# Loads of a second graph layer issued by the sync engine instead of the scalar engine, with a longer rest behind them

## The chip, the cores and the metric

The kernel runs on one core of a Trainium2 chip. A core has a tensor engine (PE, with its weight loads shown apart as PEld), a vector engine (DVE), a scalar engine (ACT), GpSimd (POOL) and a sync engine (SP). Each engine works through its own list of instructions in order; semaphores tie the lists together. DMA transfers are issued by an instruction on ACT, SP or POOL. The metric is the device time of one execution in microseconds (us): 2264.95 us before the change, the median of three runs (2263.04 to 2268.02).

## The reference, cut to what matters

A graph of 6250 nodes with 256 features and 106250 edges, sorted by their target node; 6250 of the edges are the nodes' own loops. Two layers follow one another. The first, a message network with gates, is not touched by the change. The second is an attention layer with four heads (H = 4, F = 64), called with the first one's rows:

```python
h = (x @ W).reshape(n, H, F)
a_src = jnp.sum(h * att_src[None], axis=-1)
a_dst = jnp.sum(h * att_dst[None], axis=-1)
e = jax.nn.leaky_relu(a_src[src] + a_dst[dst], 0.2)
m = jax.ops.segment_max(e, dst, num_segments=n)
ex = jnp.exp(e - m[dst])
denom = jax.ops.segment_sum(ex, dst, num_segments=n)
alpha = ex / (denom[dst] + 1e-16)
out = jax.ops.segment_sum(h[src] * alpha[..., None], dst, num_segments=n)
y = out.reshape(n, H * F) + bias + x
# layer norm with gamma and beta, relu; then x = layernorm(x + that)
```

## The kernel before, in words

**Tiles.** The edges lie in tiles of 128, one edge a partition. The loops are taken out and treated with the node itself; 782 tiles are left (`TC`). Seven tiles make a window (`WT`), 112 windows in all (`NW`), each with at most 64 target nodes (`SLOTS`). Two windows make a group, 56 groups (`NG`). For the scores, groups are taken in pairs, except the last four, 52 to 55, which stand alone (`pairs`).

**The second layer** is the block of `fast` from line 1734 on. Its main loop (line 1995) goes over steps t. At step t it emits, in this order:

- one gather on POOL (line 2002, the helper's line 1327): 128 rows of 260 numbers of the first layer's result, for the edges of tile t, into the ring `G` of ten windows;
- for tile k = t - 4, at certain places of a window, copies of the gathered logits on ACT: seven tiles of a window at its end (line 2024), the first tile of the next group for the group before (line 2016). The 112 copies of line 2024 stand in the order of the windows, so the copy of window w needs gathers 7w to 7w + 6 and all before;
- at the end of a pair, a start of `weights` (line 1807): turns the scores (line 1822), runs four scans over them for the maximum of each target's segment (lines 1829, 1830, 1839, 1840; they read `cut`), takes exponents (line 1853), and puts windows on the list `late`;
- one or two calls of `sum1` (line 1955): it takes a window of the list, weighs its rows (`weighted`: small DVE product line 1868, small ACT copy line 1873, large DVE product line 1874, which reads what line 1873 wrote), and emits one matmul that adds a tile into its group's sum (line 1983). With a group's first tile it loads that group's kept rows (line 1973, tile `k3`, ring of three). With the last it starts `finish`;
- `finish` (line 1881) works out a group's result over about a dozen steps: DVE and ACT in turn, `k3` read from line 1906 on, two layer norms (`normed`: ACT lines 1923, 1924 and 1929), then two stores by SP (line 1940), one for each window. Windows overlap, so each store waits for the one before it to land, and the first of a group waits for ACT's last line 1929 of that group.

**`Steps`** (line 1334) holds these chains. A `yield n` puts a chain to rest for n steps, in which other chains and the main loop emit their instructions. Nothing is measured in this: it is an order written down once, and each engine then follows its part of it.

**`ahead`** (line 1755) is what the change touches. For each pair it loads, for each of its groups, the slot of every edge, repeated over partitions (`dB`, two loads of 128 KB, line 1764, ring of three), and the segment marks (`cut`, line 1771, ring of three). It rests, then for each group compares `dB` with the slot numbers on DVE (line 1778), multiplies the result by the nodes' logits on PE (line 1782) and sums on DVE (line 1799). `aheads` starts it once a pair, every 28 steps (14 for the single groups). Its result is used by `weights` of the same pair, which starts 32 steps after `ahead` for a pair.

Of the kernel before, what the change touches and what calls it, by code (L numbers as in the profile page):

```python
# [1257 lines left out]
def fast(  # L1258
# [37 lines left out]
    nc = tc.nc  # L1296

    def at(ap, offset, dims):
        return bass.AP(tensor=ap.tensor, offset=ap.offset + offset, ap=dims)
# [9 lines left out]
    def windows_of(g):  # L1309
        return range(2 * g, 2 * g + 2)  # L1310
# [23 lines left out]
    class Steps:  # L1334
# [18 lines left out]
        def finish(self):  # L1353
            while self.chains:
                self.step()

    def half_of(w):
        return slice(SLOTS * (w % 2), SLOTS * (w % 2 + 1))
# [40 lines left out]
    def ring(pool, shape, dtype, name, n):  # L1399

        of = rings.setdefault((name, id(pool)), [[], 0])
        if len(of[0]) < n:
            of[0].append(pool.tile(shape, dtype, name=f"{name}_{len(of[0])}"))
        of[1] += 1
        return of[0][(of[1] - 1) % n]
# [17 lines left out]
    with (  # L1423
# [276 lines left out]
        for n in range(TC + LAG):  # L1700
            if n < TC:
                g, t = order[n]
# [19 lines left out]
            if n >= LAG:  # L1722
                g, t = order[n - LAG]
# [10 lines left out]
    with (  # L1734
# [15 lines left out]
        def tiles_in(g):  # L1750

            t0 = 2 * WT * g
            return range(t0, min(t0 + 2 * WT, TC)), range(t0, min(t0 + GS, TC))

        def ahead(pair, box):

            cut = ring(ep, [P, P + 1], F32, "cut", 3)
            of = ring(ep, [P, 2 * GS, 2 * H], F32, "of", 3)
            box.update(cut=cut, of=of)
            dBs = []  # L1760
            for g in pair:
                dB = ring(ep, [P, W8, P], BF16, "dB", 3)
                for w in windows_of(g):
                    nc.scalar.dma_start(
                        dB[half_of(w), :, :].rearrange("p j e -> p (j e)"),
                        at(slots, w * W8 * P, [[0, SLOTS], [1, W8 * P]]),
                    )
                dBs.append(dB)
            for i, g in enumerate(pair):
                n = len(tiles_in(g)[1])  # L1770
                nc.scalar.dma_start(
                    cut[i * GS * H : (i * GS + n) * H, :],
                    at(cuts, tiles_in(g)[0][0] * P, [[P, n], [0, H], [1, P + 1]]),
                )
            yield 5
            for i, (g, dB) in enumerate(zip(pair, dBs)):
                ohT = ring(ep, [P, W8, P], BF16, "ohT", 2)
                nc.vector.tensor_scalar(ohT, dB, slot_p, None, op0=OP.is_equal)
                yield 2
                pn = ring(ops, [P, 2, W8, 3, 2 * H], F32, "pn", 2)  # L1780
                for j in range(W8):
                    nc.tensor.matmul(
                        pn[:, :, j, :, :].rearrange("p s c a -> p s (c a)"),
                        ohT[:, j, :],
                        node3[:, g, :, :, :].rearrange("p s c a -> p s (c a)"),
                        start=True,
                        stop=True,
                    )
                yield 2
                o = i * GS  # L1790

                mid = pn.rearrange("p s j c a -> p (s j c) a")[:, WT * 3 : (WT + 2) * 3, :]
                n = len(tiles_in(g)[1]) - WT
                for o, parts in (
                    (o, pn[:, 0, :WT, :, :]),
                    (o + W8, pn[:, 1, 1:n, :, :]),
                    (o + WT, mid[:, None, :, :]),
                ):
                    nc.vector.tensor_reduce(
                        of[:, o : o + parts.shape[1], :],  # L1800
                        parts.rearrange("p j c a -> p j a c"),
                        axis=AX.X,
                        op=OP.add,
                    )
                yield 1
# [56 lines left out]
        def weighted(g, w, o, n, of, ex, top):  # L1862

            if g not in ohs:
                ohs[g] = ring(ep, [P, 2 * W8, SLOTS], F32, "oh1", 2)
                one_hot(ohs[g], 2 * g, 2 * W8)
            gw = ring(ep, [P, WT if n > 1 else 1, D + 2 * H], F32, f"gw{min(n, 2)}", 4)[:, :n, :]
            nc.vector.tensor_mul(  # L1868
                gw[:, :, HA:],
                top[:, o : o + n, :],  # L1870
                first[:, WT * w : WT * w + n, None].to_broadcast([P, n, H]),
            )
            nc.scalar.copy(gw[:, :, D:HA], ex[:, o : o + n, :])  # L1873
            nc.vector.tensor_mul(  # L1874
                gw[:, :, :D].rearrange("p j (h f) -> p j h f", h=H),
                of[:, :n, :D].rearrange("p j (h f) -> p j h f", h=H),
                ex[:, o : o + n, :, None].to_broadcast([P, n, H, F]),
            )
            return gw
# [73 lines left out]
        sums, queue, read, ohs, k3s, left, written = {}, [], set(), {}, {}, {}, []  # L1953

        def sum1():

            while late and len(queue) < 8:
                piece = late.pop(0)
                g, w, o, n = piece[:4]
                gw = weighted(*piece)  # L1960
                queue.extend((g, WT * w + j, gw[:, j, :]) for j in range(n))
            if not queue:
                return
            g, t, gw = queue[0]
            if g not in sums and g >= 2 and g - 2 not in read:
                return
            queue.pop(0)
            if g not in sums:
                sums[g] = ring(eps, [P, D + 2 * H], F32, "fps1", 2)
                left[g] = len(tiles_in(g)[1])  # L1970
                u = everyone
                k3s[g] = ring(fp, [P, 3, D], F32, "k3", 3)
                nc.scalar.dma_start(k3s[g][u, :, :].rearrange("p c f -> p (c f)"), kept[g, u, :])
            begins = left[g] == len(tiles_in(g)[1])
            left[g] -= 1
            j = t - 2 * WT * g
            if j == WT:
                to, ohj = everyone, ohs[g][:, WT : WT + 2, :].rearrange("p j s -> p (j s)")
            else:
                to, ohj = (slice(0, SLOTS), j) if j < WT else (slice(SLOTS, P), j + 1)  # L1980
                ohj = ohs[g][:, ohj, :]
            ends = left[g] == 0 or j in (WT - 1, TC - 1 - 2 * WT * g)
            nc.tensor.matmul(sums[g][to, :], ohj, gw, start=begins, stop=ends)  # L1983
            if left[g] == 0:
                run.start(finish(g, sums[g]), 1)

        def aheads():
            for pair in pairs:
                while run.now < 2 * WT * (pair[0] - (len(pair) == 1)):
                    yield 1  # L1990
                yield from ahead(pair, boxes[pair[0]])
# [3 lines left out]
        while t < TC + LAG or late or queue or run.chains:  # L1995
# [8 lines left out]
            if 0 <= k < TC:  # L2004
                w = k // WT
                g = w // 2
# [14 lines left out]
                if k == tiles_of(w)[0][-1]:  # L2021
# [3 lines left out]
                    if w == NW - 1:  # L2025
                        run.start(weights(pair, box))
            sum1()
            if len(queue) + W8 * len(late) > 3 * W8 or t % 7 == 0 or t >= TC - 4 * WT:
                sum1()
# [64 lines left out]
```

## Time and profile before

| | us |
|---|---|
| three runs | 2268.02, 2264.95, 2263.04 |
| the profiled execution, its own time | 2266.64 |
| its span, first to last instruction | 2264.7 |
| first gather of the second layer starts | 1213.78 |
| last gather of the second layer starts | 2198.24 |
| last instruction on POOL starts (the last store) | 2252.49 |

Busy shares of the whole span are PE 69%, DVE 55%, ACT 22% and POOL 67%. They average over two layers with different limits: in the second layer PE is busy for about half the time and DVE for three quarters. Instructions that only issue a DMA are not counted as busy[...]; the profile writes such a row with a q behind the engine's name (ACTq, SPq). A wait is written in brackets behind the instruction it held up, with the instruction that ended it.

### The profile page before, as it was taken

Reading aid. Unit: us, or ns where it says so; the run is one execution under the profiler, and the core shown is the slowest. Engines: PE = TensorE matmul, PEld = TensorE weight load, DVE = VectorE, ACT = ScalarE, POOL = GpSimd, SP = SyncE. Lnnn points to the kernel's source line nnn. Section 1 sums busy time; section 2 is a strip of 40 time slices with the busy share of each in tenths; the row PEclk is TensorE's granted clock in tenths of the full one; section 3 lists DMA queues with packets and bytes.
Section 4 is the critical chain, followed back from the end, with each engine's and each line's share of the span. In section 5 each row is a group of like instructions: output and inputs, shape, how many; then the busy total and the mean of one; then the engine's idle time right before and its main releaser. Section 6 shows DMA issues by size and latency. Waiting matters only on the chain. (4 is left out here: it accounts for less than half of the span.)

```text
span 2264.7 us, 22022 instructions
## 1 busy us (share of the span) xinstructions
PE 1556.6 (69%) x5722; PEld 776.5 (34%) x5722; DVE 1237.3 (55%) x3333; ACT 508.5 (22%) x1526; POOL 1525.5 (67%) x1603
## 2 busy tenths in 40 slices
PE   8996788888888888988992355554545545454563
PEld 5663233333333333333551222222323223232331
DVE  7552133333343333433541667777776877777785
ACT  3331012222122221222342112111111111211211
POOL 1304777777777777777764777777777777777760
PEclk9998788989999989898996676766767677676776
DMA  5335445554555554555553555555555555555540
GB/s 163 131 99 157 128 128 156 168 165 143 151 155 170 165 151 143 155 170 165 176 155 91 138 161 145 154 147 155 152 149 161 144 156 151 148 156 150 156 137 27
DMA packets 163409, 332.53 MB, mean 147 GB/s; under 512 B 42467, under 2 KB 74306, under 8 KB 163273
## 3 DMA queue, kind: packets, MB, share of 16 engines
q0 software_dynamic: 75968, 208.00, 33.9%
q1 hardware_dynamic: 64736, 82.92, 11.4%
q10 hardware_dynamic: 22569, 40.12, 5.9%
q8 instruction: 47, 0.77, 0.2%
q14 instruction: 89, 0.73, 0.1%
HBM read 278.79 MB, written 52.12 MB: 146 GB/s over the span
## 5 line engine op out<-in xcount | busy, mean ns | idle before, releaser
L1327 POOL DMA_INDIRECT G<-parts,fidx x782 | 747.1, 955 | 327.5 <-issue 219.0
L1327 POOL DMA_INDIRECT G<-rows,fidx x782 | 747.5, 956 | 240.5 <-issue 222.9
L1689 PE MATMUL fps<-G,oh 128*64 128x257 f32 (+1 forms) x1674 | 533.1, 433 | 137.1 <-DMA G<-parts,fidx 120.6
L1983 PE MATMUL fps<-gw,oh 128*64 128x264 f32 (+1 forms) x1674 | 433.0, 469 | 238.3 <-DVE gw L1874 238.3
L1983 PEld LDWEIGHTS fps<-gw,oh 128*64 128x64 f32 (+1 forms) x1674 | 229.1, 168 | 412.8 <-DVE gw L1874 254.8
L1689 PEld LDWEIGHTS fps<-G,oh 128*64 128x64 f32 (+1 forms) x1674 | 196.6, 151 | 445.5 <-DMA G<-parts,fidx 226.7
L1874 DVE TENSOR_TENSOR gw<-G,bank 128x1792 f32<-128x1792 f32 (+1 forms) x167 | 249.0, 1491 | 175.0 <-ACT gw L1873 173.5
L1495 DVE TENSOR_SCALAR kind<-fps 128x1 f32<-128x1 f32 x112 | 12.5, 153 | 311.1 <-PE fps L1689 311.1
L1542 PE MATMUL fpg<-faT,fWihT 128*128 128x512 f32 (+2 forms) x432 | 171.6, 521 | 0.2 <-DVE faT L1513 0.2
L1822 PE MATMUL turn<-fident,e 128*120 128x128 f32 (+2 forms) x30 | 13.5, 449 | 219.4 <-ACT e L2016 219.4
L1410 DVE TENSOR_TENSOR oh<-bank,fslot 128x1024 f32<-128x1024 f32 x112 | 136.0, 1214 | 2.2 <-ACT bank L1853 2.2
L1923 ACT ACTIVATE frs<-fmv,eps_c 128x1 f32<-128x1 f32 x112 | 33.0, 294 | 306.0 <-DVE fmv L1922 152.0
L1650 DVE COPY nd<-hr 128x4 f32<-128x4 f32 x56 | 10.8, 193 | 160.1 <-ACT hr L1629 160.1
L1205 PE MATMUL fpm<-fWrT,fhT 128*128 128x256 f32 x392 | 91.7, 388 | 5.1 <-DVE fms L1213 5.1
L1542 PEld LDWEIGHTS fpg<-faT,fWihT 128*128 128x128 f32 x432 | 71.2, 191 | 68.9 <-issue 59.3
L1191 PE MATMUL fph<-fxc,fWrT 128*128 128x512 f32 (+1 forms) x208 | 88.9, 580 | 4.7 <-DMA fWrT<-in_WrT_dram 4.7
L1929 ACT ACTIVATE fy<-fy,frs 128x256 f32<-128x256 f32 x112 | 67.2, 600 | 98.4 <-DVE gw L1868 52.9
L1822 PEld LDWEIGHTS turn<-fident,e 128*120 128x120 f32 (+2 forms) x30 | 5.0, 166 | 233.2 <-ACT e L2016 231.6
L1205 PEld LDWEIGHTS fpm<-fWrT,fhT 128*128 128x128 f32 x392 | 74.9, 194 | 23.8 <-DVE fms L1213 8.8
L1873 ACT COPY gw<-bank 128x28 f32<-128x28 f32 (+1 forms) x167 | 28.5, 171 | 227.6 <-DMA dB<-slots 103.6
L1625 PE MATMUL fpg<-Wx,fyT 128*128 128x264 f32 x224 | 77.0, 474 | 3.0 <-ACT fyT L1616 3.0
L937 POOL DMA_INDIRECT packed<-frame,place x21 | 20.9, 995 | 77.6 <-DVE frame L902 71.5
(237 smaller groups left out, 1791.3 us busy)
## 6 DMA issues: line engine op xcount, KB each, us to landing
kept<-keep SPq DMA_DIRECT2D x56, 384.0 KB
k<-kept ACTq DMA_DIRECT2D x56, 384.0 KB
dB<-slots ACTq DMA_DIRECT2D x112, 128.0 KB
loop<-parts SPq DMA_DIRECT2D x110, 128.0 KB
parts<-fms SPq DMA_DIRECT2D x49, 256.0 KB
G<-parts,fidx POOLq DMA_INDIRECT x782
G<-rows,fidx POOLq DMA_INDIRECT x782
rows<-hr SPq DMA_DIRECT2D x110, 65.0 KB
```

The lines of the kernel that those rows point to most:

```text
L1191: nc.tensor.matmul(ph[:, :cols], WrT_s[:, r, k, m * P : (m + 1) * P], xc[:, k, :cols], start=(k == 0), stop=(k == 1),)
L1205: made = nc.tensor.matmul(pm[:, r, :], hT[:, r, k, j * P : (j + 1) * P], WrT_s[:, r, k, :], start=(k == 0), stop=(k == 1),)
L1327: nc.gpsimd.indirect_dma_start(out=to_tile, out_offset=None, in_=table, in_offset=bass.IndirectOffsetOnAxis(ap=idx, axis=0),)
L1410: nc.vector.tensor_tensor(to[:, :nj, :], iota_s[:, None, :].to_broadcast([P, nj, SLOTS]), of[:, :, None].to_broadcast([P, nj, SLOTS]), op= ...
L1542: nc.tensor.matmul(pg[:, :cols], WihT_s[:, k, c * P : (c + 1) * P], aT[:, k, :cols], start=(k == 0), stop=(k == 1),)
L1625: nc.tensor.matmul(ph[u, :], hs[i][:, k, u], Wx[:, k, :], start=(k == 0), stop=(k == 1))
L1689: nc.tensor.matmul(sums[g][to, :], ohj, got[t], start=begins, stop=ends)
L1873: nc.scalar.copy(gw[:, :, D:HA], ex[:, o : o + n, :])
L1874: nc.vector.tensor_mul(gw[:, :, :D].rearrange("p j (h f) -> p j h f", h=H), of[:, :n, :D].rearrange("p j (h f) -> p j h f", h=H), ex[:, o ...
L1923: nc.scalar.activation(r, mv[u, k, 1:2], AF.Ln, bias=eps_c[u])
L1929: nc.scalar.activation(y, y, AF.Identity, bias=m, scale=r)
L1983: nc.tensor.matmul(sums[g][to, :], ohj, gw, start=begins, stop=ends)
```

## The change

Three load instructions move from the scalar engine's list to the sync engine's: the slots (line 1764, 112 loads), the segment marks (line 1771, 56 loads) and the kept rows (line 1973, 56 loads). The rest behind the loads in `ahead` grows from 5 steps to 8. No line is added, so the line numbers stay.

```diff
@@ ahead @@
                 for w in windows_of(g):
-                    nc.scalar.dma_start(
+                    nc.sync.dma_start(
                         dB[half_of(w), :, :].rearrange("p j e -> p (j e)"),
                         at(slots, w * W8 * P, [[0, SLOTS], [1, W8 * P]]),
                     )
...
                 n = len(tiles_in(g)[1])
-                nc.scalar.dma_start(
+                nc.sync.dma_start(
                     cut[i * GS * H : (i * GS + n) * H, :],
                     at(cuts, tiles_in(g)[0][0] * P, [[P, n], [0, H], [1, P + 1]]),
                 )
-            yield 5
+            yield 8
@@ sum1 @@
                 k3s[g] = ring(fp, [P, 3, D], F32, "k3", 3)
-                nc.scalar.dma_start(k3s[g][u, :, :].rearrange("p c f -> p (c f)"), kept[g, u, :])
+                nc.sync.dma_start(k3s[g][u, :, :].rearrange("p c f -> p (c f)"), kept[g, u, :])
```

## The prediction

> **What bounds the kernel now.** The chain of waits came first; it stops at the last store and tells nothing. Then came busy time by stretch (columns: length, PE, PEld, DVE, ACT, POOL, each with its count, granted clock, DMA share, GB/s) and who waited for whom from 1250 us on (us in total, times, longest).
>
> ```profile
> by line: POOL out_dram L1942 0.0%; issue 0.0%; POOLq L1244 0.0%
> ...
> 1400.00:1600.00 200.00, 100.90 (x458) 56.78 (x459) 151.83 (x381) 38.22 (x157) 151.56 (x160) 0.68 0.55 150
> 1800.00:2000.00 200.00, 103.01 (x464) 57.84 (x464) 150.53 (x375) 38.16 (x156) 151.69 (x159) 0.70 0.56 152
> ...
> DVE gw L1874 <- ACT gw L1873: 173.5, 152, 5.2
> ACT gw L1873 <- DMA dB<-slots: 103.6, 25, 4.5
> POOL G L1327 <- issue: 213.3, 700, 0.3
> ```
>
> POOL makes 160 gathers in each 200 us, one per 1.25 us, and never waits over 0.3 us: in the second layer it runs at its own pace. All 782 gathers take from 1213.78 to 2199.19 us (last start 2198.24 plus 0.95), 985.41 us, 1.260 each, so 35.28 us for a pair's 28. What follows the last gather, 65.5 us to the end of the span, is DVE, ACT and PE catching up. The question is how far behind they are, and why. Lines of the timeline (start, duration), two of POOL's each with the ACT copy of line 2024 that needs it:
>
> ```profile
> 1433.32 1.19 POOL L1327 DMA_INDIRECT G<-rows,fidx  x1 [0.30 <-issue]
> 1436.51 0.21 ACT L2024 COPY e<-G 128x28 f32<-128x28 f32 x1 [0.34 <-DMA G<-rows,fidx]
> ...
> 2103.41 0.95 POOL L1327 DMA_INDIRECT G<-rows,fidx  x1 [0.30 <-issue]
> 2116.95 0.21 ACT L2024 COPY e<-G 128x28 f32<-128x28 f32 x1
> ...
> 2198.24 0.95 POOL L1327 DMA_INDIRECT G<-rows,fidx  x1 [0.30 <-issue]
> ...
> 2223.85 0.19 ACT L2024 COPY e<-G 128x20 f32<-128x20 f32 x1
> ```
>
> Counted in order, the first two are gather 174 and the copy of window 24: the copy starts 2.0 us after the gather ended (1434.50), waiting for its data. The next two are gather 706 and window 100: 12.6 us behind (2104.35 to 2116.95), waiting for no data. The last two are gather 781 and window 111: 24.7 us behind. So DVE and ACT are a little slower than POOL and lose 10.6 us in the 19 pairs from window 24 to 100 (0.56 a pair), then 12.1 in the single groups. Pairs confirm it: ACT's first slot load of two successive pairs starts at 2034.84 and 2070.57, 35.73 us apart against 35.28. Why they are slower shows in one pair:
>
> ```profile
> 2034.78 0.20 ACT L1924 ACTIVATE frs<-frs 128x1 f32<-128x1 f32 x1
> 2034.84 2.46 ACTq L1764 DMA_DIRECT2D dB<-slots  x4
> ...
> 2037.33 1.83 ACTq L1771 DMA_DIRECT2D cut<-cuts  x2
> ...
> 2039.20 0.16 ACT L1873 COPY gw<-bank 128x4 f32<-128x4 f32 x1 [4.22 <-DMA dB<-slots]
> 2039.40 0.42 DVE L1874 TENSOR_TENSOR gw<-G,bank 128x256 f32<-128x256 f32 x1 [4.93 <-ACT gw L1873]
> ```
>
> ACT issues six loads in a row, 4.3 us, and a 0.16 us copy stands behind them; DVE, which has nothing else it may do, idles 4.93 us for that copy. The same wait comes in 25 pairs (103.6 us). DVE is the busiest of the three followers, so the idle time is lost.
>
> **The Trainium skill.** "DMA: Bandwidth & Descriptors", Issuing engines are not separate DMA queues: transfers from any engine share the same 16 DMA engines, and another issuer saves only its sequencer's time to initiate, "which is usually small relative to the DMA itself". Here the trace differs on small: 4.3 us of issue a pair is what holds DVE. "Perfetto Trace Analysis", DMA Instruction — HWDGE: a load's profiled duration ends when the sequencer is free again, and leaves out the movement of data. The trace agrees: in the packets of ACT's queue a slot load's last one ends 1.7 us after the start of issue (3.1 at worst), a kept-rows load's 3.1 (4.9), against these issue times (min, median, max in ns):
>
> ```profile
> L1764 ACTq DMA_DIRECT2D dB<-slots x112: 473/602/620, 1213.2 to 2182.1; - x112
> L1771 ACTq DMA_DIRECT2D cut<-cuts x56: 822/892/1443, 1215.7 to 2182.6; - x56
> L1973 ACTq DMA_DIRECT2D k<-kept x56: 321/327/347, 1263.3 to 2236.6; - x56
> ```
>
> **The change, part by part.**
>
> *Removed from ACT:* 112 x 0.60 + 56 x 0.89 + 56 x 0.33 = 67 + 50 + 18 = 135 us of issue. Most of it is no path: only what made DVE wait counts. In a pair that is 4.93 less the 0.70 that the same wait costs where only the small copy and its neighbours stand there: 4.2 us. A pair then takes DVE and ACT 35.73 - 4.2 = 31.5 us, under POOL's 35.28. They catch up with every pair and wait for gathers instead; the lag stays at the 2.0 us of window 24. At window 100 that is 10.6 us less.
>
> *In the single groups* the same loads (about 2 us a group) held DVE at 2144.65 (2.62 for a usual 0.70) and at 2158.62 (1.18 for a usual 0.15): 1.9 + 1.0 = 2.9 us. The issues at 2127 and 2181 held no DVE work. Sum 13.5 us.
>
> *Given back:* with less lag, data are late again. Window 104's copy (2150.75), moved 12.5 us earlier, would stand at 2138.25, but its last gather ends at 2139.67 and needs the usual 2.0: 3.4 us short. ACT's next instruction (2154.70) waits 3.73 us for DVE anyway, which covers it: nothing if the cover holds, 3.4 if not. I take 1.0, estimated, for this and the like. Net 12.5 us.
>
> *Added to SP:* a pair gets 4 slot loads, 2 mark loads and 2 kept-row loads, at ACT's durations 2.4 + 1.8 + 0.7 = 4.9 us, beside four stores of 0.47. SP issues nothing else there and mostly waits:
>
> ```profile
> SPq L1940 <- ACT fy L1929: 287.5, 29, 20.4
> ```
>
> I price SP's issue by ACT's; the bounds are 0.33 us (the cheapest row above) and twice ACT's, and neither fills a pair. What matters is what each load stands behind. In the built order of the changed kernel a pair's loads follow the second store of an odd group and one kept-rows load. That store ended its issue at 2032.60 in this pair; with 0.33 for kept rows and 1.1 for the first group's two slot loads all is issued by 2034.1, where ACT only began at 2034.84. Landing is by 2036.6 at the worst 3.1 us. The first comparison (line 1778) ran at 2042.55; without the stall it would run at 2038.3, and the longer rest places it behind four more DVE instructions (lines 1829, 1830, 1836, 1837, 1.4 us). Some 3 us to spare. Kept rows of group g follow the stores of group g - 2; their first use (line 1906) comes 12 to 22 us after those stores in the pairs, against 3.1 to land (4.9 at worst); in the single groups they stand there or a store earlier. A store that is late behind loads holds up nothing nearer than the reuse of its buffer three groups on.
>
> *The longer rest* costs no instruction; it moves lines 1778, 1782 and 1799 three or more steps later. Cover: a pair's results are used 32 steps after its loads, and `ahead` ends at step 18 instead of 15. A single group's `ahead` ends at most 17 steps after its due time, where its `weights` starts 32 after. The first pair's results are due after 32 gathers, 40 us. If that cover failed, each late step would cost one gather, 1.26 us.
>
> *The end* is in the same order: only line 1799's and 1778's places move, none of them behind the last `weights`. After the last copy 40.8 us follow, unchanged. Span 2264.7 - 12.5 = 2252.2. The profiled execution took 2266.64 in its own time, 1.7 over the median of 2264.95; the same 12.5 from the median gives **2252.5 us**.
>
> **Rivals.**
>
> *Larger gain.* The lag vanishes in the single groups too, from 24.7 to 2.0: 22.7 us, 2242. For it: ACT is freed throughout. Against: from window 100 to 111 the followers took 106.9 us for 94.8 us of gathers, and only 2.9 of the 12.1 excess is load issue.
>
> *No change.* POOL hides the middle and the freed time turns into another wait, such as line 1929's on DVE behind the copy; then only the 2.9 us of the single groups remain: 2262, within 0.2% (4.5 us), about what a measurement of this kernel tells from nothing. Against: in the pair shown, ACT's copy needs nothing that is late; its exponents are from long before.
>
> *Slower.* A store waiting on SP holds the slot loads behind it, and DVE's line 1778 waits W us a pair for them, with `weights` and the sums behind it. The margin of a pair is 35.28 - 31.5 = 3.8 us, so below W = 3.8 nothing is lost, at 4.3 it equals the kernel before, and from about 4.6 it is slower by over 0.2%. At W = 6 the lag grows 2.2 us in each of 25 pairs to 56, against 10.6 before, less the 2.9 of the single groups: 2307. For it: SP's waits for a result last up to 20.4 us. Against: loads would have to be 7 us later than worked out, and no unfinished store stands between.
>
> *It does not do what it says:* excluded, the built order shows the loads on SP and gone from ACT.
>
> **How the numbers follow.** Forecast 0.75, with its own range 2248 to 2257 (gain 14.5 to 10 by the cover above and up to a further 0.5 a single group from kept-row issue, and 2 us of scatter as in the three runs). Larger 0.08. Smaller gain, 5 to 9 us, 0.05. No change 0.04. Slower 0.08. Faster by over 0.2% is 0.75 + 0.08 + 0.05 = 0.88. From 2245 to 2259 takes the forecast, half of the larger case and most of the smaller: 0.75 + 0.04 + 0.03 = 0.82.
>
> **What would show it.** ACT has no line 1764; DVE's wait for line 1873 falls from 173.5 by about 100 us; the copy of window 100 starts some 2 to 4 us after its gather, that of window 111 some 11 to 13 after; gathers still take 985 us; the stretch from that last copy to the end is still 41 us. Wrong would be: waits of DVE line 1778 for slot loads or of line 1906 for kept rows, a lag that still grows, or gathers that wait over 0.3 us.

## The result, and the profile after

The changed kernel took 2252.2 us (median of five runs, 2250.4 to 2254.72) beside 2265.71 us for the kernel before (now five runs, 2263.04 to 2268.85): ratio 0.994 [0.9925, 0.9954], 13.5 us less. 2252.5 was predicted. The profiled execution took 2252.2 in its own time; its span is 2250.4, against 2264.7 before.

First, who waited for whom in the second layer (us in total, times, longest; from 1250 us on). The first line is of the kernel before, the others of the changed one:

```profile
ACT e L2024 <- DMA G<-rows,fidx: 43.6, 23, 8.5
...
ACT e L2024 <- DMA G<-rows,fidx: 240.7, 80, 8.4
POOL G L1327 <- issue: 215.4, 707, 0.3
DVE frs L1926 <- ACT frs L1924: 75.1, 32, 4.5
DVE gw L1874 <- ACT gw L1873: 62.2, 141, 2.5
```

DVE's wait for the small copy fell from 173.5 to 62.2 us. ACT's window copies now wait for gathers 80 times, 240.7 us in all, where they did so 23 times before. The followers, DVE and ACT, have become faster than POOL and wait for it. POOL itself still waits for nothing over 0.3 us, and its count in a stretch of 200 us is unchanged (length, PE, PEld, DVE, ACT, POOL, clock, DMA share, GB/s):

```profile
1400.00:1600.00 200.00, 104.47 (x472) 57.08 (x472) 154.13 (x385) 38.61 (x160) 151.56 (x160) 0.69 0.54 149
```

The place itself, in one pair of the timeline (start, duration):

```profile
2056.36 2.42 SPq L1764 DMA_DIRECT2D dB<-slots  x4
...
2058.13 0.20 ACT L1924 ACTIVATE frs<-frs 128x1 f32<-128x1 f32 x1
2058.24 0.14 ACT L1873 COPY gw<-bank 128x4 f32<-128x4 f32 x1
2058.41 0.42 DVE L1874 TENSOR_TENSOR gw<-G,bank 128x256 f32<-128x256 f32 x1 [0.60 <-ACT gw L1873]
2058.82 1.85 SPq L1771 DMA_DIRECT2D cut<-cuts  x2
```

ACT goes from line 1924 straight to the copy, which before started at 2039.20, when the sixth load's issue had just ended (2037.33 + 1.83 = 2039.16). DVE waits 0.60 us instead of 4.93, while SP issues the six loads beside it. The copies of windows 100 and 111, each with the last gather that it needs:

```profile
2101.75 0.95 POOL L1327 DMA_INDIRECT G<-rows,fidx  x1 [0.30 <-issue]
2104.60 0.21 ACT L2024 COPY e<-G 128x28 f32<-128x28 f32 x1 [1.68 <-DMA G<-rows,fidx]
...
2196.11 0.95 POOL L1327 DMA_INDIRECT G<-rows,fidx  x1 [0.30 <-issue]
...
2210.05 0.19 ACT L2024 COPY e<-G 128x20 f32<-128x20 f32 x1
```

The first starts 1.9 us after the gather ended (2102.70), waiting for its data; before it was 12.6. The last starts 13.0 us after (2197.06); before 24.7. This distance, a copy's start less the end of its last gather, is called the lag below.

So the 14.3 us of span are: 11.7 of lag at the last window, 2.1 from a last gather that ended earlier (the first gather began 0.5 earlier, and all of them together took 1.7 less), 0.5 in what follows the last copy. In the profiles of four kernels below with a like lag (slots only, marks only, half the marks, the old rest) the last gather ended anywhere from 2195.7 to 2202.5, so I count the 2.1 as scatter of single executions and not as the change's work.

### The profile page after: what moved, and what is told of

Its sections match the earlier page's. It is cut to its first block, busy times and chain, and to the rows that moved or that the text cites. A ratio compares the mean times of both kernels' runs of the same rounds, so it can differ in the third digit from the quotient of the medians.

```text
span 2250.4 us, 22097 instructions
## 1 busy us (share of the span) xinstructions
PE 1553.1 (69%) x5722; PEld 768.8 (34%) x5722; DVE 1242.7 (55%) x3333; ACT 506.0 (22%) x1526; POOL 1524.7 (68%) x1603
## 5 line engine op out<-in xcount | busy, mean ns | idle before, releaser
L1327 POOL DMA_INDIRECT G<-rows,fidx x782 | 745.8, 954 | 240.7 <-issue 225.4
L1983 PE MATMUL fps<-gw,oh 128*64 128x264 f32 (+1 forms) x1674 | 438.9, 469 | 249.1 <-DVE gw L1874 249.0
L1874 DVE TENSOR_TENSOR gw<-G,bank 128x1792 f32<-128x1792 f32 (+1 forms) x167 | 248.9, 1490 | 65.2 <-ACT gw L1873 62.2
L1495 DVE TENSOR_SCALAR kind<-fps 128x1 f32<-128x1 f32 x112 | 12.5, 153 | 314.1 <-PE fps L1689 314.0
L2024 ACT COPY e<-G 128x28 f32<-128x28 f32 x112 | 23.9, 214 | 268.3 <-DMA G<-rows,fidx 267.7
```

The source lines that it names most:

```text
L1327: nc.gpsimd.indirect_dma_start(out=to_tile, out_offset=None, in_=table, in_offset=bass.IndirectOffsetOnAxis(ap=idx, axis=0),)
L1874: nc.vector.tensor_mul(gw[:, :, :D].rearrange("p j (h f) -> p j h f", h=H), of[:, :n, :D].rearrange("p j (h f) -> p j h f", h=H), ex[:, o ...
L2024: nc.scalar.copy(box["e"][:, o : o + own, :], G[w][:, :own, D:HA])
```

## Experiments

The theory: DVE and ACT lose to POOL only because ACT issues six loads in front of one small copy; once a pair takes the followers less than POOL's 35.28 us, the rest of the freed time is worth nothing. The rivals: it is ACT's total load, or the queue that the loads stand in, or the longer rest. Ratios are to the kernel before, run beside each; the profiles give the lag.

### Each part alone

**Slots only:** line 1764 alone goes to SP, the rest stays 5.

```diff
-                    nc.scalar.dma_start(
+                    nc.sync.dma_start(
```

> Only the slot loads go to SP; marks, kept rows and the rest of 5 stay. Theory A (a threshold: the followers lose 0.5 us a pair on POOL, and anything over that taken off ACT's block brings them back to POOL's pace): ACT's block in a pair falls from 4.2 to some 1.8 us, the copy of window 100 starts 2 to 4 us after its gather, some 11 us gained, 2254 to 2256. Theory B (the gain goes with the issue time removed, 67 of 135 us): half of 13.5, 2259. Theory C (the longer rest makes the gain): 2265.

Measured: 2256.59 us, 0.9959 [0.9945, 0.9972]; lag 3.2 at window 100, 12.1 at window 111. The kernel before took 2267.48 us beside it, so the gain is 10.9 us, as theory A has it. The half of 13.5 that theory B expects lies just inside the interval, so this run alone does not decide; the next two exclude B.

**Marks only:** line 1771 alone.

```diff
-                nc.scalar.dma_start(
+                nc.sync.dma_start(
```

> Only the segment marks go to SP. Theory A: the block falls from 4.2 to 2.5 us, still more than 0.5 saved, so the lag at window 100 is 2 to 5 us and the gain some 10 to 11 us, 2254 to 2257. Theory B (50 of 135 us): 5 us, 2261. Theory C: 2265.

Measured: 2253.95 us, 0.9946 [0.9932, 0.996]; lag 2.1 and 11.7. In its waits seven tenths of DVE's idle time for the copy are left, and the time is still that of the whole change:

```profile
DVE gw L1874 <- ACT gw L1873: 123.6, 139, 4.2
ACT gw L1873 <- DMA dB<-slots: 40.5, 17, 2.8
```

**Half the marks:** only the second of a pair's two mark loads, 0.9 us of ACT's 4.3.

```diff
-                nc.scalar.dma_start(
+                (nc.sync if i else nc.scalar).dma_start(
```

> Only the mark load of a pair's second group goes to SP, 0.9 us of the block of 4.2; the single groups keep theirs. Theory A (a threshold of some 0.5 us a pair): lag 2 to 5 us at window 100, 9 to 10 us gained, the single groups' 3 not, 2256 to 2259. Theory B (in proportion to the issue removed, 24 of 135 us): 2264.

Measured: 2254.51 us, 0.9952 [0.9938, 0.9965]. ACT's copy still waits behind the loads 25 times (in 24 pairs and one single group), by up to 3.5 us, and window 100 still waits for its data (waits, then timeline):

```profile
DVE gw L1874 <- ACT gw L1873: 148.7, 144, 4.2
ACT gw L1873 <- DMA dB<-slots: 80.4, 25, 3.5
...
2103.81 0.95 POOL L1327 DMA_INDIRECT G<-rows,fidx  x1 [0.30 <-issue]
...
2106.67 0.21 ACT L2024 COPY e<-G 128x28 f32<-128x28 f32 x1 [1.94 <-DMA G<-rows,fidx]
```

Lag 1.9 at window 100, 13.0 at 111. Removing 0.9 us a pair gives about as much as removing 4.3, because the followers were only 0.55 us a pair too slow: a threshold, and not a gain in proportion.

**Kept rows only:** line 1973.

```diff
-                nc.scalar.dma_start(k3s[g][u, :, :]...
+                nc.sync.dma_start(k3s[g][u, :, :]...
```

> Only the kept rows go to SP. They are not in ACT's block of six; one of two a pair stands ahead of a copy of line 1873 and costs DVE 0.70 for 0.15, 0.55 us a pair, about what the followers lose. Theory A: the lag grows little or not, 3 to 8 us at window 100, 2257 to 2263. Theory B (18 of 135 us): 1.8 us, 2263.5. Theory C: 2265.

Measured: 2267.33 us, 1.0 [0.9992, 1.0008]; lag 11.4 and 22.7. The wait of the copy is what it was before (173.5):

```profile
DVE gw L1874 <- ACT gw L1873: 173.3, 156, 5.2
```

18 us less issue on ACT, and nothing came of it. The expectation was missed: DVE's waits of 0.7 us for the copy, which it put down to these loads, were 46 before and are 48 now, so something else causes them, and the loads of the kept rows held nobody up.

### The longer rest alone

```diff
-            yield 5
+            yield 8
```

> All loads stay on ACT, the rest is 8 steps. Theories A and B: no issue is removed, ACT's block of six stays, lag about 12 us at window 100, 2263 to 2267. Theory C (the later place of lines 1778 to 1799 shortens the followers' pair): the lag is 2 to 4 us, 2252 to 2256.

Measured: 2281.84 us, 1.007 [1.0056, 1.0084]: some 14 us slower than before, which none of the theories had. The lag is 29.7 at window 100 (timeline, with the gather that it needs) and 41.7 at 111:

```profile
2102.19 0.95 POOL L1327 DMA_INDIRECT G<-rows,fidx  x1 [0.30 <-issue]
...
2132.89 0.21 ACT L2024 COPY e<-G 128x28 f32<-128x28 f32 x1
```

Between the copies of windows 60 and 100, ten pairs, the lag grew by 1.30 us a pair (16.7 to 29.7), where the kernel before lost 0.55 (7.1 to 12.6): 0.75 us a pair more. Two of DVE's waits have grown (the first two lines are of the kernel before, the others of this one):

```profile
DVE frs L1926 <- ACT frs L1924: 7.7, 27, 0.6
DVE oh L1410 <- ACT bank L1853: 2.2, 3, 1.6
...
DVE frs L1926 <- ACT frs L1924: 18.2, 31, 0.6
DVE oh L1410 <- ACT bank L1853: 9.1, 27, 2.1
```

That is 10.5 and 6.9 us more, 17.4 together; the lag at window 111 is 17.1 greater. The timelines show where the first comes from. Before the change the first comparison of a pair stood between lines 1922 and 1926, where DVE waits for ACT's lines 1923 and 1924 anyway:

```profile
2113.95 0.18 DVE L1922 BATCH_NORM_AGGREGATE fmv<-fst 128x2 f32<-128x6 f32 x1
2114.05 0.56 DVE L1778 TENSOR_SCALAR ohT<-dB,slot_p 128x1024 bf16<-128x1024 bf16 x1
2114.73 0.16 DVE L1926 SCALAR_TENSOR_TENSOR frs<-fmv,frs 128x1 f32<-128x1 f32 x1
```

With the longer rest and nothing else:

```profile
2129.72 0.18 DVE L1922 BATCH_NORM_AGGREGATE fmv<-fst 128x2 f32<-128x6 f32 x1
...
2130.49 0.16 DVE L1926 SCALAR_TENSOR_TENSOR frs<-fmv,frs 128x1 f32<-128x1 f32 x1 [0.60 <-ACT frs L1924]
...
2131.89 0.48 DVE L1778 TENSOR_SCALAR ohT<-dB,slot_p 128x1024 bf16<-128x1024 bf16 x1
```

The comparison no longer fills that hole: DVE idles 0.60 us there and does the 0.48 us later. In 24 pairs of the kernel before, the first comparison stood in this place, and in none with a rest of 8. The second comparison of a pair, which stood behind line 1840, now stands ahead of lines 1848 to 1851, from which line 1853 takes its input; that is the likely reason why line 1410 waits longer for the exponents, but no run tests it alone.

### The loads on SP without the longer rest

Lines 1764, 1771 and 1973 go to SP, and the rest stays 5.

```diff
-                    nc.scalar.dma_start(
+                    nc.sync.dma_start(
```

> All loads on SP as in the changed kernel, but the rest stays at 5. By the prediction's working the slot loads land 1.7 us before their use even so. Theory A: no wait of DVE on slot loads that POOL's margin does not cover, lag 2 to 4 us at window 100, 2249 to 2254, the longer rest was not needed. Rival (the rest hides the loads' landing behind SP's stores): DVE's line 1778 waits for slot loads in most pairs, 2256 or more.

Measured: 2254.89 us, 0.9954 [0.994, 0.9968]; lag 3.7 and 10.5. This can't be told from the changed kernel. The rival's sign, waits of line 1778 in most pairs, came in five of them and was small:

```profile
DVE ohT L1778 <- DMA dB<-slots: 2.8, 5, 1.0
```

The loads only just arrive: from the second pair on, the last packet of a pair's first slots ends 1.2 us or more before the comparison starts, with the rest of 8 at least 4.6. The rest of 8 was not needed for the gain, nor did it visibly spoil it: in the pairs the 0.75 us that it costs has room in the time in which DVE and ACT wait for POOL. In the single groups, where they are still the slower side, it may cost something: the lag at window 111 is 10.5 with 5 steps and 13.0 with 8. What follows the last copy is 1.2 us longer with 5, so some 1.4 us are left of that, from one profile of each.

### All loads on ACT, but not in one block

Nothing goes to SP. A step lies between the loads, so that the copy is emitted among them, and the rest is cut by as many steps.

```diff
                 dBs.append(dB)
+                yield 1
             for i, g in enumerate(pair):
+                if i:
+                    yield 1
                 ...
-            yield 5
+            yield 5 - (2 * len(pair) - 1)
```

> All loads stay on ACT with their full 135 us of issue, but a step lies between a group's slot loads and the next loads, and the rest is cut by as many steps, so that comparisons stand where they stood. Theory A (what counts is the block of six in front of one small copy): pieces of 1.2 or 0.9 us hide mostly in ACT's idle time, lag 2 to 5 us at window 100, 2253 to 2259. Rival (ACT's total issue time counts, or the queue that the loads are on): 2265 or more.

Measured: 2253.24 us, 0.9948 [0.9934, 0.9961]; lag 2.0 and 11.7. The timeline of one pair (here line 1876 is the copy, 1877 the product, 1774 the marks):

```profile
2063.36 1.17 ACTq L1764 DMA_DIRECT2D dB<-slots  x2
2064.58 0.16 ACT L1876 COPY gw<-bank 128x4 f32<-128x4 f32 x1 [1.07 <-issue]
2064.60 1.22 ACTq L1764 DMA_DIRECT2D dB<-slots  x2
2064.77 0.42 DVE L1877 TENSOR_TENSOR gw<-G,bank 128x256 f32<-128x256 f32 x1 [1.78 <-ACT gw L1876]
2065.95 0.90 ACTq L1774 DMA_DIRECT2D cut<-cuts  x1
2067.85 0.89 ACTq L1774 DMA_DIRECT2D cut<-cuts  x1
```

Two loads stand ahead of the copy instead of six, DVE waits 1.78 us, and the gain is the same with all 135 us of issue left on ACT. So neither ACT's total nor the queue was the cause, but what stood in front of one copy. A kernel that must keep SP free could have had nearly 12 us this way.

### The block made longer

The kernel before, with each slot load issued twice; the second goes into a tile that nobody reads.

```diff
+                dX = ring(ep, [P, W8, P], BF16, "dX", 3)
...
+                    for to in (dB, dX):
-                    nc.scalar.dma_start(dB[half_of(w), ...
+                        nc.scalar.dma_start(to[half_of(w), ...
```

> The kernel before with each slot load issued a second time on ACT, into a tile that nobody reads: 2.5 us more in the block of each pair. Theory A: all of it is on the path, since the followers are already the slower side: pair 38.3 us, the lag at window 100 grows to some 65 us unless POOL has to wait for its ring first, 2265 + 25 x 2.5 = 2325 (2310 to 2335). Rival (ACT's issue is hidden behind POOL): 2265 to 2270.

Measured: 2330.22 us, 1.0288 [1.0272, 1.0304], 65.3 us more than the kernel before. Its waits (lines shifted by two):

```profile
DVE gw L1876 <- ACT gw L1875: 235.5, 145, 7.8
POOL G L1327 <- DVE gw L1876: 44.9, 14, 3.3
```

DVE's wait for the copy grew from 173.5 to 235.5 us, by 62.0, which is nearly all of the 65.3: on this side of the threshold the time follows the block about one for one. (The doubled loads also move more data; that leaves little for it to have cost.) The second line is new: the followers are so far behind that POOL, the pace until now, waits for a free window of its ring. The lag stands at 38.4 from window 60 on.

Put in one row, loads in ACT's block of a pair against the time: 6.7 us, 2330; 4.3, 2265; 3.4, 2254.5; 2.5, 2254; 1.9, 2256.6; none, 2252 to 2255 (the kernel before took 2264.9 to 2267.5 beside them). It is a slope of about one above 4.3, and flat from 3.4 down. No run lies between; the 0.55 us a pair that the kernel before lost puts the bend at some 3.7 us, an estimate.

### The single groups, the rest and the pairs: not settled

Four kernels were run together on another chip, where the kernel before itself took 3064.93 us (67 runs, 3044 to 3083), so that what they say holds for that condition alone. The changed kernel itself was not run there.

Only the single groups' loads on SP (line 1764; line 1771 likewise):

```diff
-                    nc.scalar.dma_start(
+                    (nc.sync if len(pair) == 1 else nc.scalar).dma_start(
```

> Slot and mark loads go to SP for the four single groups alone; the pairs' stay on ACT, kept rows too, rest 5. By the prediction's working: lag at window 100 as before, 12 to 13 us, and 2.9 us less after it, 2262 (2260 to 2264). Rival (the end of the layer is where the gain is made): 2253 to 2258.

Measured: 3064.53, 1.0 [0.9977, 1.0024]. The interval, some 7 us either way, is too wide for the 2.9 us in question.

The changed kernel with a rest of 1:

```diff
-            yield 8
+            yield 1
```

> The changed kernel with a rest of 1 step instead of 8: the comparisons come 7 steps (8.8 us) earlier, where by the prediction's working slot loads have just been issued. Theory A: DVE waits for slot loads in each pair, about 1 to 4 us, which POOL's margin of 3.8 us a pair covers; 2250 to 2260. The rival of the prediction on the slower side (loads late on SP) decides if these waits pass the margin: lag grows from pair to pair, over 2265.

Measured: 3084.65, 1.0059 [1.004, 1.0078]: some 20 us slower than the kernel before in that condition, where the two kernels that follow, with their loads on SP too and the rest of 8, are not.

The changed kernel with two single groups at the end, and with none:

```diff
-    pairs = [[g, g + 1] for g in range(0, NG - 4, 2)] + [[g] for g in range(NG - 4, NG)]
+    pairs = [[g, g + 1] for g in range(0, NG - 2, 2)] + [[g] for g in range(NG - 2, NG)]
```

> The changed kernel with two single groups at the end instead of four (the groups before them as a pair), so two runs of the scores' scans fewer where the followers fall behind (lag 4.5 us at window 104, 13.0 at 111). If DVE's work is what grows this lag: some 6 us less work, 2246 to 2251. If the end hangs on how late the last scores start: 2252 to 2258.

```diff
+    pairs = [[g, g + 1] for g in range(0, NG, 2)]
```

> The changed kernel with pairs to the end. Less work still for DVE, but the last pair's scores start only after all gathers, and four windows are weighed after that: 2252 to 2265; below 2250 if only DVE's work counts.

Measured: 3061.53, 0.9994 [0.9977, 1.0012], and 3065.4, 0.9999 [0.998, 1.0019].

There the second layer has another limit. In the waits of the first of the four, from 1900 to 2900 us:

```profile
DVE s L1829 <- remote: 353.5, 19, 18.8
POOL G L1327 <- DVE gw L1874: 352.3, 18, 19.7
```

DVE's first scan of a pair waits 18.6 us on average for something that this view only calls remote, and POOL, with its ring full, waits for DVE: the copy's lag is 70 to 71 us from window 24 to 104. ACT's block is still there (4.21 us before the copy at 2432.28); the last two kernels, which have no such block, are no faster, so the block does not look like what sets the pace there. The trace's record of the scan names one semaphore, which PE raises: it waits for PE and not for the marks. With the rest of 1 a wait as long (370.1 us in 18 cases) stands at line 1799, for the same semaphore. PE's matmuls that come before are recorded as ended some 18 us earlier, and what held PE the records do not show. So the worth of the single groups' loads by themselves, and of other rests and pairings, stays open.

## Why the prediction was right, and where not

**The main step held.** "ACT issues six loads in a row, 4.3 us, and a 0.16 us copy stands behind them", so that a pair "under POOL's 35.28" lets the followers catch up. Lag at window 100: 2.0 predicted, 1.9 measured; a difference of 10.7 us for the 10.6 of the sum. Half the marks and the doubled slots show both sides of the bend, and the spread loads show that it is the place and not the amount. (The "25 pairs" of the forecast are 24 pairs and one single group; the sum does not hang on it.) The forecast set the trace against the word "small" that it quotes. For a single load the two agree, 0.60 us of issue to 2.9 until the last packet's end; it was six in a row ahead of one copy that cost.

**Its size was not needed.** The forecast took 4.2 us out of a pair, and 0.55, an eighth, was all that a pair could give; the rest became waiting for gathers, as the forecast said.

**Single groups:** 2.9 less 1.0 "given back" was to leave 1.9 us. From window 100 to 111 the lag grew 12.1 before and 11.1 after: 1.0 us. The place named for giving back was right: the copy of window 104 waited for its data (7.44 us in the timeline). It started 4.5 us after the end of the gather, not the 2.0 that the forecast took as usual. ACT's next instruction started at 2142.64, against 2142.2 by the forecast's shift, so there the wait cost 0.4 us beyond its cover. Two profiles with the rest of 5 say more. With half the marks, where the single groups' loads stay on ACT, the lag at window 111 was 13.0; with all loads on SP it was 10.5, 2.5 less for the 2.9 of the forecast. With the rest of 8 it is 13.0 again. So the longer rest probably took back in the single groups what the moved loads gave there. These are single profiles, whose stretches after the last copy differ by up to 1.2 us, and it is not shown. Altogether the lag gave 11.7 where 12.5 was forecast. The median fell by 13.5, with an interval of some 10 to 17, which holds both. That it came within 0.3 us of the forecast is luck: the lag gave 0.8 less, and in the profiled execution the gathers and the stretch after the last copy gave 2.6 that were not forecast.

**Kept rows:** the forecast removed their 18 us from ACT as "no path", and the single run of them agrees. But it priced SP's issue by ACT's, and for these that was off once all three kinds of load were on SP: 0.48 us for 0.33. Alone on SP they took 0.33 too. The first two lines are of the changed kernel, the third is of the run of the kept rows alone:

```profile
L1764 SPq DMA_DIRECT2D dB<-slots x112: 444/596/922, 1212.9 to 2161.5; - x112
L1973 SPq DMA_DIRECT2D k<-kept x56: 319/482/593, 1221.6 to 2216.9; - x56
...
L1973 SPq DMA_DIRECT2D k<-kept x56: 320/332/587, 1214.6 to 2230.4; - x56
```

The slot loads cost the same on both (0.596 for 0.602). Line 1906 never waits for kept rows in the second layer, and line 1778 waits for slots once, 6.3 us, with the first loads of the layer.

**Landing:** the forecast read 1.7 us (3.1 at worst) from the start of a slot load's issue to the end of its last packet. Counted as 64 packets a load in the order of their start, that trace gives 2.9 (3.8 at worst), so the "3 us to spare" were some 2.3 by the same working. In the changed kernel's pair shown above the first group's slots were in by 2060.34, 5.6 us before the comparison at 2065.92, so the error did no harm.

**The longer rest was the term that failed.** "The longer rest costs no instruction; it moves lines 1778, 1782 and 1799 three or more steps later", and the cover named was that the results are used 32 steps after the loads. That cover held, and it was the wrong question. A moved instruction leaves a hole where it stood: line 1778 had filled a 0.60 us wait of DVE for ACT. Alone the longer rest costs 14 us. In the changed kernel its cost can't be seen, because the other edit put DVE and ACT under POOL's pace in the pairs. The forecast had the margin (3.8 us a pair) and did not name it as the cover. That the first comparison stood between lines 1922 and 1926 could be read in the trace of the kernel before.

**The rivals.** The larger gain did not come: the single groups are still slower than their gathers. No change is outside the interval. Slower needed W above 3.8 us in the pairs; W was nothing. Of the signs named, the wait for line 1873 fell by 111 for "about 100", the gathers took 983.7 us for 985, and what follows the last copy 40.4 for 41.

The Trainium skill's page "Perfetto Trace Analysis", in Optimization Strategy, advises to find the gaps on the engine that bounds a stretch and what blocks it there. In this trace POOL, with the even pace, has no gap over 0.3 us to find; DVE, as busy as POOL (151.83 and 151.56 of 200 us), has one of 4.93 us in a pair, and following it back leads to ACT's six loads. How much of it counted, 0.55 us, showed only in the distance between the two engines.

## What to carry to other kernels

Where one engine sets a steady pace and others follow, measure how far behind the followers are at several points: whether the distance grows tells which side sets the end, and its growth in one round (here 0.55 us a pair) is all that a round can gain on the followers' side. DMA issues hurt by where they stand: here a block in front of a short instruction that another engine waits for cost its whole length while that engine was the slower side, and nothing once it had time to spare or the same loads were spread out. And an instruction moved "at no cost" may have been filling a wait; look at what stands on both sides of its old place.

## What was not expected of the hardware

On one chip both layers of this kernel ran slower, 3065 us for 2265 (mean granted clock 0.72 in the profile against 0.81), with a repeated wait of 18.6 us at one DVE instruction. No gain was seen there from what was tried, and the bound was another; the change as a whole was not among it.

An issue of the same kept-rows load took 0.33 us on ACT and alone on SP, and 0.48 us on SP beside the slots and marks (0.47 with the rest of 5). So it is not the engine that makes the difference but the company; how, no run shows. The slot loads took 0.60 on both engines.
